# One relu of each unit of the last stage moved from VectorE to ScalarE, in a two-layer bottleneck network

## The chip, the cores and the metric

The kernel runs on one core of a Trainium2 chip. The metric is the device time of one execution in microseconds; the median of three runs of the kernel before is 1983.51 us (1981.97 to 1983.78). The profile is of one further execution of 1982.28 us, with a span of 1980.2 us from the first to the last instruction. Engines are called PE (TensorE, the matrix multiplier; PEld is its weight load), DVE (VectorE), ACT (ScalarE), POOL (GpSimd) and SP (SyncE, which here only queues transfers).

## The reference

Two layers of the same form follow each other, on x of 64 images, 1024 channels, 14 x 14 pixels, in fp32. Each is a bottleneck block with batch statistics taken over the whole batch:

```python
out = jax.nn.relu(_bn(_conv(x, w1, b1, 1, 0), g1, be1))     # 1x1, 1024 -> 256
out = jax.nn.relu(_bn(_conv(out, w2, b2, 1, 1), g2, be2))   # 3x3, 256 -> 256
out = _bn(_conv(out, w3, b3, 1, 0), g3, be3)                # 1x1, 256 -> 1024
out = jax.nn.softplus(residual_scale)[0] * out
out = x + out
return jax.nn.relu(out)
```

The change lies in the last lines of the second layer: third convolution, scale and shift of its normalisation, addition of x, relu, output.

## The kernel before

The batch is cut into T = 32 tiles of two images. A tile of x is 128 partitions x 8 channel blocks x 392 pixels, 1568 KB. The first layer's result lies in device memory (`mid`); the last stage reads it as x, adds the third convolution of the second layer and writes `out`.

The 1x1 convolutions are made with a scheme of seven products in place of eight for a 2 x 2 block of sub-products (`Seven`). In the last stage (`final`, `Conv3Pair`) one **unit** takes a pair of tiles (t, t + 1) and two output channel blocks, `o[0]` = q and `o[1]` = q + 4. Its four results are called (row, i): row picks the channel block, i the tile. A pair has four units (q = 0 to 3), and there are 15 pairs, so 60 units; tile 0 and tile 31 are done by plain products (`residual`) before and after.

A unit has seven products, p1 to p7, of two matmuls each. Three PSUM banks take them: cy (p1, then p6, p7 and p4 added on top), cx (p2), cp (p5, then p3 on top). Between the products the bank is read:

- after p1 and after p6 ACT saves cy, scaled, into the two halves of `cu12`; after p7 into `cu3` (line 438, by way of `act`, line 320);
- DVE adds a scaled bank to x in place (`add`, line 446): (0,0) after p2, (1,1) after p5, (0,1) after p3, (1,0) after p4;
- POOL adds `cu3` to (1,1) (line 467) and the halves of `cu12` to (0,0) and (0,1) (line 493).

So p3 of a unit can't start until DVE has read cp after p5, and p4 not until ACT has read cy after p7.

`stream` (line 294) interleaves each unit with the one before it: p1 of the new unit, p3 and p4 of the old one, then p6 of the new one, then `end()` of the old one, then p2, p5 and p7 of the new one. In `end()` ACT does the relus of row 0, (0,0) and (0,1), with the shift as its bias. The relus of row 1 are in `go_out`, by DVE as add and max in one instruction (line 504). `go_out` is called by the loop `while len(units) > 2` after a later unit's p7, so that a unit is finished two units after its own products. It also queues the unit's two output transfers on SP, one for each tile i, each with two channel blocks (392 KB, line 508).

Before the first unit of a pair DVE makes the column sums t1 to t4 of the pair's inputs (`column_sums`, lines 410 to 413); t1 and t2 have one buffer, t3 and t4 two. x tiles have five buffers. After a pair's second unit the loads of two more tiles are queued (line 1133); each needs a buffer that all four outputs of an earlier tile have left.

The order of ACT's instructions and that of line 504 is held as written (`keep_in_program_order`); the other adds, the column sums, POOL's work and the transfers are placed by the compiler's scheduler.

Of the kernel before, what the change touches and what calls it, by code (L numbers as in the profile page):

```python
# [39 lines left out]
ALU = mybir.AluOpType  # L40
# [47 lines left out]
def bottlenecks(ctx: ExitStack, tc: tile.TileContext, x, w1s, w2s, w3s, pars, out):  # L88
    nc = tc.nc
# [228 lines left out]
    def act(*args, **kw):  # L318

        tc.keep_in_program_order(nc.scalar.activation(*args, **kw))  # L320

    class Conv1(Seven):
# [33 lines left out]
        def end(self):  # L356
            if self.ts[-1] == T - 1 - len(self.ts):
                summarize(self.stats, T // 2 - 1, T - len(self.ts), PX)
# [124 lines left out]
    class Conv3Pair(Conv3):  # L483
# [9 lines left out]
                nc.gpsimd.tensor_add(v, v, self.u12[:, i * self.n : (i + 1) * self.n])  # L493

        def end(self):
            for i in range(2):
                o, v = self.o[0], self.part(0, i)
                act(v, v, AF.Relu, bias=self.shift[:, o : o + 1])

        def go_out(self):  # L500
            for i in range(2):
                o, v = self.o[1], self.part(1, i)
                tc.keep_in_program_order(
                    nc.vector.tensor_scalar(v, v, self.shift[:, o : o + 1], 0.0, ALU.add, ALU.max)  # L504
                )
            q, step = self.o[0], CS // 2
            for i in range(2):
                nc.sync.dma_start(
                    out=self.to[i].rearrange("p (s f) -> p s f", s=CS)[:, q::step, :], in_=self.xt[i][:, q::step, :]
                )  # L510
# [28 lines left out]
    def conv2(psum, pool, b, par, aff, affine_of, stats):  # L539
# [23 lines left out]
        def rows(g, s, k, first, end):  # L563

            return y_grp[:, s, g, 4 * first + k - 1 : 4 * end + k - 4 : 4, :]
# [226 lines left out]
        def finish():  # L792


            for g in range(NG):
# [43 lines left out]
                end = y_grp[:, :, g, H - 1]  # L839
                nc.vector.tensor_add(out_rows[3], d3, fa[:, :, :full])  # L840
                nc.vector.tensor_add(end, d[:, :, full], fa[:, :, full])
                stat(0, [out_rows[3][:, o] for o in range(MS)])
                stat(1, [end[:, o] for o in range(MS)])
# [114 lines left out]
    def gram(psum, pool, homes, aff, minus_c, beside):  # L958
# [17 lines left out]
        def norm_to(end):  # L976

            while pieces and pieces[0][0] < end:
                a, e = pieces.pop(0)
                for s in reversed(range(MS)):  # L980
                    y = y_all[:, s, a:e]
                    if a == 0 and s == 1:
                        norm_vector(s, y, aff, minus_c[:, s : s + 1])
                    else:
                        norm(s, y, aff)
                        less(s, y)
# [422 lines left out]
```

## Time and profile before

| | |
|---|---|
| median of three runs | 1983.51 us |
| profiled span | 1980.2 us |
| PE busy | 1926.9 us, 97% |
| DVE busy | 1582.8 us, 80% |
| ACT busy | 1017.1 us, 51% |
| POOL busy | 540.6 us, 27% |
| granted TensorE clock, mean | 0.991 |

Over the last stage, between 1700 and 1960 us:

| us busy of 260 | PE | DVE | ACT | POOL | DMA share |
|---|---|---|---|---|---|
| | 255.95 | 235.88 | 150.66 | 176.41 | 0.93 |

In that stretch the costliest groups are: DVE line 504, 110 relus, mean 806 ns; DVE line 446, 217 adds, mean about 620 ns; ACT line 320, 164 saves of cy with a mean of 585 ns and 109 relus with a mean of 613 ns; POOL line 493, 109 adds, mean 1042 ns, and line 467, 55 adds, mean 1179 ns.

How to read this: PE's busy share overstates what it does, since matmuls overlap; the distance from one matmul's start to the next says more. A line number can be that of a helper: every ACT instruction of this stage has line 320 and every matmul line 168, so the names of the tiles tell which is which (`x<-x,shift` is a relu, `cu<-cy,scale` a save). In a timeline row, the first number is the start, the second the length of the row (several instructions of one kind make one row, with their count after x), and a bracket gives the idle time of the engine before it and what ended it.

### The profile page before, as it was taken

What the parts mean: (1) busy time and instruction counts of PE and PEld (TensorE: products, weight loads), DVE (VectorE), ACT (ScalarE), POOL (GpSimd) and SP (SyncE); (2) the same over time, 40 slices, a digit from 0 to 9 for tenths busy, and PEclk for the clock granted to TensorE, in tenths of its full rate; (3) what the DMA queues carried; (4) which work ended last, traced back from release to release, by engine and by line L of the source; (5) the groups of instructions that cost most, each with busy time, mean ns of one, the idle gap of its engine ahead of it and who ended that gap; (6) DMA issues with size and microseconds to landing.
All of it is one profiled execution on the core that took longest, in us unless ns stands there. A gap on an engine that the chain in (4) does not pass through costs nothing.

```text
span 1980.2 us, 27057 instructions
## 1 busy us (share of the span) xinstructions
PE 1926.9 (97%) x9432; PEld 1619.1 (82%) x9432; DVE 1582.8 (80%) x2554; ACT 1017.1 (51%) x2039; POOL 540.6 (27%) x638
## 2 busy tenths in 40 slices
PE   8999998999998999999999999989999899999998
PEld 5555557999997789999999999979999887555555
DVE  5778758999997566776776776699999974888997
ACT  1222214677765055555555555447777631555555
POOL 0111100000105133433433433201010060666665
PEclk9999999999999999999999999999999999999999
DMA  7776724676748534444444444257676385799998
GB/s 291 272 255 241 256 98 154 182 209 194 201 138 211 186 131 171 186 165 171 185 165 171 184 167 171 90 183 203 201 192 203 117 209 210 248 330 333 342 335 298
DMA packets 188983, 408.39 MB, mean 206 GB/s; under 512 B 24944, under 2 KB 165136, under 8 KB 172336
## 3 DMA queue, kind: packets, MB, share of 16 engines
q1 hardware_dynamic: 161728, 324.66, 47.8%
q0 software_dynamic: 21504, 30.94, 6.7%
q10 hardware_dynamic: 5616, 51.06, 6.1%
q8 instruction: 75, 1.23, 0.2%
q14 instruction: 60, 0.49, 0.1%
HBM read 263.75 MB, written 115.34 MB: 191 GB/s over the span
## 4 chain that ended last, share of the span: by engine, by line
PE 84%; DVE 10%; DMA 3%; issue 1%; ACT 1%; POOL 0%; DVEq 0%; SPq 0%; ACTq 0%
PE ay L168 17%; PE cy L168 14%; PE columns L168 11%; PE cp L168 11%; PE ap L168 10%; PE m L168 5%; PE l L168 5%; PE ax L168 5%; PE cx L168 4%; DMA x<-mid 2%; DVE x L446 2%; DMA out<-x 1%; PE ps L168 1%; DVE x L504 1%; DVE f L782 1%
## 5 line engine op out<-in xcount | busy, mean ns | idle before, releaser
L320 ACT ACTIVATE cu<-cy,scale 128x196 f32<-128x196 f32 (+1 forms) x552 | 256.9, 474 | 298.7 <-PE cy L168 291.4
L168 PE MATMUL columns<-v,ub 128*128 128x224 f32 (+1 forms) x1536 | 302.1, 338 | 0.7 <-ACT columns L741 0.7
L168 PEld LDWEIGHTS columns<-v,ub 128*128 128x128 f32 x1536 | 270.4, 189 | 4.4 <-ACT columns L741 1.2
L320 ACT ACTIVATE x<-x,shift 128x392 f32<-128x392 f32 x368 | 211.6, 614 | 68.5 <-POOL x L472 52.8
L446 DVE SCALAR_TENSOR_TENSOR x<-cp,scale,x 128x196 f32<-128x196 f32 (+1 forms) x368 | 178.1, 484 | 84.2 <-PE cp L168 81.3
L168 PE MATMUL cy<-ct,ws 128*128 128x196 f32 (+1 forms) x736 | 221.7, 383 | 2.5 <-ACT cu L320 2.5
L467 POOL TENSOR_TENSOR x<-x,cu 128x196 f32<-128x196 f32 (+1 forms) x184 | 167.7, 912 | 170.8 <-ACT cu L320 170.4
L168 PE MATMUL ay<-at,ws 128*128 128x196 f32 (+1 forms) x752 | 209.3, 381 | 1.0 <-ACT au L320 1.0
L472 POOL TENSOR_TENSOR x<-x,cu 128x392 f32<-128x392 f32 x124 | 125.9, 1015 | 190.7 <-DVE x L446 185.9
L168 PEld LDWEIGHTS ay<-at,ws 128*128 128x128 f32 x752 | 136.3, 190 | 35.1 <-ACT au L320 1.9
L168 PEld LDWEIGHTS cy<-ct,ws 128*128 128x128 f32 x736 | 133.6, 190 | 37.0 <-ACT cu L320 4.1
L168 PE MATMUL l<-diffs,ub 128*128 128x224 f32 (+1 forms) x768 | 149.6, 338 | 5.6 <-issue 3.2
L168 PE MATMUL m<-sums,ua 128*128 128x224 f32 (+1 forms) x752 | 145.9, 337 | 3.1 <-DVE sums L607 3.1
L493 POOL TENSOR_TENSOR x<-x,cu 128x392 f32<-128x392 f32 x120 | 125.0, 1042 | 84.1 <-DVE x L446 75.1
L852 POOL DMA_DIRECT2D y<-f x24 | 31.1, 1533 | 411.7 <-DVE f L782 411.7
L168 PEld LDWEIGHTS l<-diffs,ub 128*128 128x128 f32 x768 | 133.7, 189 | 9.6 <-PE columns L168 5.0
L168 PEld LDWEIGHTS m<-sums,ua 128*128 128x128 f32 x752 | 131.3, 189 | 4.9 <-DVE sums L607 4.5
L320 ACT ACTIVATE au<-ay 128x196 f32<-128x196 f32 (+1 forms) x141 | 53.6, 380 | 158.2 <-PE ay L168 157.6
L446 DVE SCALAR_TENSOR_TENSOR x<-cx,scale,x 128x196 f32<-128x196 f32 (+1 forms) x184 | 89.2, 485 | 52.0 <-PE cx L168 51.8
L168 PE MATMUL cy<-y,w 128*128 128x196 f32 (+1 forms) x404 | 126.8, 400 | 0.0
L168 PE MATMUL cx<-y,w 128*128 128x196 f32 (+1 forms) x404 | 125.3, 396 | 0.0
L168 PE MATMUL cp<-zt 128*128 128x257 f32 x392 | 120.1, 388 | 1.7 <-DVE zt L1010 1.7
(203 smaller groups left out, 3990.4 us busy)
## 6 DMA issues: line engine op xcount, KB each, us to landing
x<-in_x SPq DMA_DIRECT2D x62, 1568.0 KB, 6.9
ub<-u SPq DMA_DIRECT2D x94, 768.0 KB, 5.3
x<-mid SPq DMA_DIRECT2D x32, 1568.0 KB, 10.3
mid<-x ACTq DMA_DIRECT2D x31, 1568.0 KB, 5.1
out<-x SPq DMA_DIRECT2D x123, 392.0 KB, 6.9
ua<-u SPq DMA_DIRECT2D x94, 256.0 KB, 3.0
u<-y POOLq DMA_DIRECT2D x48, 256.0 KB, 6.0
home<-y SPq DMA_DIRECT2D x90, 96.0 KB, 4.0
```

The costliest lines, as they stand in the source:

```text
L168: tc.keep_in_program_order(nc.tensor.matmul(*args, **kw))
L320: tc.keep_in_program_order(nc.scalar.activation(*args, **kw))
L446: nc.vector.scalar_tensor_tensor(v, bank, self.scale[:, o : o + 1], v, ALU.mult, ALU.add)
L467: nc.gpsimd.tensor_add(self.part(1, 1), self.part(1, 1), u3)
L472: nc.gpsimd.tensor_add(v, v, self.u12)
L493: nc.gpsimd.tensor_add(v, v, self.u12[:, i * self.n : (i + 1) * self.n])
L504: nc.vector.tensor_scalar(v, v, self.shift[:, o : o + 1], 0.0, ALU.add, ALU.max)
L782: nc.vector.tensor_add(to, v, ls)
L852: nc.gpsimd.dma_start(out=out_rows[0][:, o], in_=f[:, o], accum_op=ALU.add)
```

## The change

The relu of (1,1) leaves `go_out` and DVE and goes to `end()` and ACT, ahead of the two that are there; that of (1,0) stays. It is meant to take work off DVE, which is busier than ACT in this stage.

```diff
         def end(self):
-            for i in range(2):
-                o, v = self.o[0], self.part(0, i)
+            for row, i in (1, 1), (0, 0), (0, 1):
+                o, v = self.o[row], self.part(row, i)
                 act(v, v, AF.Relu, bias=self.shift[:, o : o + 1])
 
         def go_out(self):
-            for i in range(2):
-                o, v = self.o[1], self.part(1, i)
-                tc.keep_in_program_order(
-                    nc.vector.tensor_scalar(v, v, self.shift[:, o : o + 1], 0.0, ALU.add, ALU.max)
-                )
+            o, v = self.o[1], self.part(1, 0)
+            tc.keep_in_program_order(nc.vector.tensor_scalar(v, v, self.shift[:, o : o + 1], 0.0, ALU.add, ALU.max))
             q, step = self.o[0], CS // 2
             for i in range(2):
                 nc.sync.dma_start(
```

## The prediction

> **What bounds the kernel now.** I looked for the stage, then its waits, then the order of work inside one pair of x tiles. The change touches the last stage alone: the VectorE relu of line 504 runs 120 times from 1689.9 to 1967.2 us, two for each of 60 units. The busy table of a stretch that holds exactly 12 pairs (four units each):
>
> ```profile
> 1711.72:1942.93 231.21, 227.30 (x673) 124.63 (x672) 209.70 (x337) 133.07 (x241) 156.16 (x145) 1.00 0.94 332
> ```
>
> Columns: length, PE, PE weight loads, DVE, ACT, POOL, granted clock, DMA share, GB/s. In undisturbed rows of the timeline four matmuls start within 1.32 us, 0.329 each, so 673 need 221.4 of the 231.2 us: PE loses 9.8 us here, 0.82 a pair. DVE is busy 91%, ACT 58%. DMA is busy 231.21 x 0.94 / 12 = 18.1 us a pair; 56 matmuls need 18.42; a pair takes 19.27. So PE leads, and DMA is close behind. Who waits, 1695 to 1960 us (total us, times, longest):
>
> ```profile
> ACT cu L320 <- PE cy L168: 92.0, 88, 2.1
> POOL x L493 <- DVE x L446: 72.4, 79, 1.7
> PEld cp L168 <- DVE x L446: 20.8, 28, 1.4
> ACT x L320 <- POOL x L493: 13.8, 23, 0.9
> ...
> POOL x L493 <- DMA x<-mid: 5.2, 4, 1.3
> ```
>
> The third row costs PE time: twice in each of 14 pairs the weights of p3, which accumulates into bank cp, wait until DVE's add (line 446) after p5 has read that bank. By the last row an x tile came late in 4 pairs. DVE's timeline where the next pair's column sums (lines 410 to 413) fall due:
>
> ```profile
> 1866.03 0.82 DVE L411 TENSOR_TENSOR ct<-ct,y 128x392 f32<-128x392 f32 x1
> 1866.88 0.57 DVE L413 TENSOR_TENSOR ct<-y,ct 128x392 f32<-128x392 f32 x1
> ...
> 1868.44 2.03 DVE L504 TENSOR_SCALAR x<-x,shift 128x392 f32<-128x392 f32 x2
> 1870.39 0.55 DVE L412 TENSOR_TENSOR ct<-y 128x392 f32<-128x392 f32 x1
> 1870.87 0.61 DVE L446 SCALAR_TENSOR_TENSOR x<-cp,scale,x 128x392 f32<-128x392 f32 x1
> 1871.40 0.55 DVE L410 TENSOR_TENSOR ct<-y 128x392 f32<-128x392 f32 x1
> ...
> 1872.95 0.61 DVE L446 SCALAR_TENSOR_TENSOR x<-cp,scale,x 128x392 f32<-128x392 f32 x1
> ```
>
> In other units two relus take 1.14 us and DVE then idles 0.29. Here there are two losses. The first follows lines 411 and 413 with no relu between; by the starts of consecutive matmuls PE loses 0.22 us. The second follows relus of 2.03 us: the p5 add starts at 1872.95 instead of about 1872.17 (p5's matmuls start at 1871.31, and in the undisturbed unit before, matmuls at 1861.87 had their add at 1862.73, 0.86 later), and PE loses 0.41. Over the 14 pairs I count 14 x 0.22 = 3.1 us; nine second losses of about 0.41, 3.7; four of 0.88 to 1.04 where the tile was late as well, 3.8; 0.3 at the end; together 11. The tile's path is in the chain of waits:
>
> ```profile
> 1877.84 0.74 DVE x L504
> 1878.62 5.53 DMA out<-x
> 1884.29 6.63 DMA x<-mid
> 1891.00 1.65 DVE x L446 x3
> ```
>
> A relu frees the output transfer, its landing frees a buffer, the load fills it, and an add of the next pair's first unit uses it. Here the load landed at 1890.92, when the add was just about due: this path has next to no slack. The sync queue:
>
> ```profile
> 1859.54 5.14 SPq L508 DMA_DIRECT2D out<-x  x3
> 1864.85 1.05 SPq L123 DMA_DIRECT2D x<-mid  x2
> 1866.00 17.76 SPq L508 DMA_DIRECT2D out<-x  x8
> ```
>
> In the code the two loads (line 1133) stand ahead of the next unit's two outputs; here they sit between these two. So transfers are queued when they become ready, not as written.
>
> **What the Trainium skill says.** "SBUF — State Buffer", section "Who interferes with whom": a one-source DVE instruction in its two-port mode and a GpSimd instruction exclude each other for the whole instruction; a DVE instruction with two SBUF inputs is excluded by a GpSimd read. The trace agrees: line 504 takes from 0.41 to 1.18 us, mean 0.81, and line 411 takes 0.83 against 0.55 for line 412. "ScalarE: Activation LUTs", section "What ACT_TABLE_LOAD costs": 280 ns + 0.833 ns per element for an activation with a bias column, less some 93 ns back to back, so 606 ns for 392. The trace has 613, and pairs of relus in 1.12: 0.51 for each further one. "VectorE: DVE Perf Modes", section "Mode 2×_2P", lets an fp32 tensor-scalar in SBUF use both ports, which the 0.41 us of the fastest relu fits.
>
> **The change part by part.**
> 1. DVE loses 60 relus, 60 x 0.81 = 48 us of its time, 3.2 a pair. Only what precedes the second loss is on PE's path; elsewhere DVE idles afterwards. There the queue becomes: p5 add, one relu, line 412, p3 add. The saving isn't half of 2.03. GpSimd's add of line 467 runs 1869.10 to 1870.24; line 412 has two SBUF inputs and would now arrive during it, to end at about 1870.6 instead of 1870.94. So the saving is 0.33 us at least, and 1.17 (the second relu whole) if GpSimd isn't in the way. I take 0.33: the p5 add comes at 1872.62, 0.45 late instead of 0.78, and the loss shrinks from 0.41 to 0.08.
> 2. The first loss of 0.22 stays.
> 3. ACT gains 60 relus of 0.51 = 31 us, 58% to 70% of the stage. In an undisturbed unit it runs cu at 1861.42, relus at 1861.90 and 1862.41, and idles 0.37 until cu after p7 at 1863.39. The third relu starts at 1862.92 and ends that slot at 1863.43, so this cu is 0.04 us late. Behind it wait GpSimd's line 467 and PE's p4, whose weights need cu by some 0.2 us after its end: hidden. The relu of (1,1) goes first and waits for line 467 of its unit, done at 1865.29, 1.2 us before its turn: nothing. The relu that waited for GpSimd (13.8 us) is now third, half a microsecond later: no cost.
> 4. Output transfer i = 1 no longer needs DVE. Its last input is the relu of (0,1), ready at about 1863.5 for a unit whose transfer goes out now after the relu of line 504 over a unit later. By the order seen above it will be queued when ready, some 5 us earlier (one unit of 4.6 and a bit), and that tile's buffer is free as much earlier. The first load can take it; it then lands well ahead of its add. The four late tiles lose their excess too: 0.96 becomes 0.08.
>
> Sum: 9 x 0.33 + 4 x 0.88 = 3.0 + 3.5 = 6.5 us. 1983.5 - 6.5 = **1977.0 us**. A pair would then take 18.42 + 0.30 = 18.7 us, above DMA's 18.1. The end (last residual tile on PE, a final output of 1.9 us) keeps its length.
>
> **The rivals.**
> - A, above: 0.62; its bounds for the second loss (0 or 0.2 left) give 1976.0 to 1978.6.
> - E, the first loss goes too, since with less to do DVE runs its sums earlier: all of 10.6 saved, 1973. For it: lines 412 and 410 already run early when inputs allow; against: line 411 starts 0.2 us after the last p6 that read its old value. 0.06.
> - B, the transfers keep their order: loads land just in time as now, and 18.1 us of DMA plus the wait for a landing hold a pair near 19.0. Then about 0.2 us of each of 9 pairs, 1981.7. For it: transfers of 3 to 14 us show a standing backlog. 0.10.
> - C, GpSimd's lock, not the relu, holds DVE: lines 412 and 410 wait as long as the relu did, and only the late tiles improve, 4 x 0.55 = 2.2, 1981.3. 0.06.
> - D, slower. The sync queue has one place in a pair where it stands until a landing, both loads behind it. If the loads come apart, it has two. An output takes 2.8 us from issue to landing at best, but about 1.1 each in a backlog: up to 1.7 us of empty DMA at a wait. With half of that at each of two, a pair takes 18.1 + 1.7 = 19.8 us, 0.5 above today: 14 x 0.5 = 7, 1990.5. For it: DMA's 94%; against: two outputs queued behind the awaited one fill the hole. 0.16.
>
> **How the numbers follow.** 0.2% is 4.0 us, so faster means below 1979.5: nearly all of A, E and a little of B, 0.67. Same: the rest of B and C, and what of A falls short, 0.16. Slower: D and the worst of B, 0.17. The range leaves out D and the far side of E: 1974.0 to 1984.0.
>
> **What would show it.** Right: line 504 x60 and line 320's relu x428; PE's wait of cp weights for line 446 at about 14 large times instead of 28, longest under 0.6; no wait for x<-mid; outputs i = 1 ahead of outputs i = 0; a pair at 18.7 us. Wrong: PE waiting for ACT's cu (0.6 us now), line 412 or 410 growing by what the relu gave up, or long waits of the sync queue for landings with DMA's share falling while x<-mid is late.

## The result and the profile after

The changed kernel takes 1976.78 us, the median of four runs (1975.40 to 1977.39), against 1983.64 us for the kernel before, measured beside it (four runs, 1981.97 to 1984.72). The ratio is 0.9965, with an interval of 0.9948 to 0.9982: faster by 6.9 us, with 3.6 to 10.3 inside the interval. A later repetition gave 1976.81 us against 1982.40, ratio 0.9972 [0.9962, 0.9982]. The forecast was 1977.0.

I read the stage in the same order as before. First the busy table of twelve pairs, the same columns: length, PE, PE weight loads, DVE, ACT, POOL, granted clock, DMA share, GB/s. A pair has 56 matmuls, so a stretch with 672 of them is twelve pairs:

```profile
1711.40:1937.00 225.60, 225.42 (x672) 124.89 (x671) 188.59 (x288) 152.47 (x288) 146.75 (x145) 1.00 0.94 334
```

A pair takes 225.60 / 12 = 18.80 us (19.27 before, 18.7 forecast). DVE is busy 84% of the time (91% before), ACT 68% (58%). DMA's share is the same 0.94, so the same bytes go out in less time.

The waits in the stage, 1690 to 1955 us (total us, times, longest):

```profile
ACT cu L320 <- PE cy L168: 76.7, 56, 1.6
POOL x L493 <- DVE x L446: 65.3, 76, 1.7
DVE x L446 <- PE cp L168: 21.4, 43, 0.6
...
PEld cp L168 <- DVE x L446: 15.6, 28, 0.8
ACT x L320 <- POOL x L493: 4.5, 13, 0.4
PEld cy L168 <- ACT cu L320: 4.1, 13, 0.3
POOL x L493 <- DMA x<-mid: 1.5, 1, 1.5
```

DVE now waits for PE (third row, 43 times; 7.9 us in 27 before), which is how an engine with time to spare looks. PE's wait for DVE before p3 is still there 28 times, twice in each of 14 pairs, but shorter: 15.6 us for 20.8. One x tile came late where four had. The page of the changed kernel has the relu of ACT with its new count, 428 instead of 368:

```profile
L320 ACT ACTIVATE x<-x,shift 128x392 f32<-128x392 f32 x428 | 240.9, 613 | 58.2 <-POOL x L472 52.5
```

DVE's queue where the next pair's column sums fall due, with GpSimd's line 467 and the p5 matmuls between (start, length, engine, line, operation):

```profile
1842.87 0.83 DVE L411 TENSOR_TENSOR ct<-ct,y 128x392 f32<-128x392 f32 x1
1843.73 0.57 DVE L413 TENSOR_TENSOR ct<-y,ct 128x392 f32<-128x392 f32 x1
...
1845.29 0.93 DVE L502 TENSOR_SCALAR x<-x,shift 128x392 f32<-128x392 f32 x1
...
1845.95 1.13 POOL L467 TENSOR_TENSOR x<-x,cu 128x392 f32<-128x392 f32 x1
1846.13 1.38 DVE L412 TENSOR_TENSOR ct<-y 128x392 f32<-128x392 f32 x1
...
1847.43 0.55 DVE L410 TENSOR_TENSOR ct<-y 128x392 f32<-128x392 f32 x1
...
1848.16 0.82 PE L168 MATMUL cp<-ct,ws 128*128 128x392 f32 x2
...
1848.60 2.14 POOL L493 TENSOR_TENSOR x<-x,cu 128x392 f32<-128x392 f32 x2 [1.52 <-DVE x L446]
...
1849.51 0.61 DVE L446 SCALAR_TENSOR_TENSOR x<-cp,scale,x 128x392 f32<-128x392 f32 x1
```

One relu of 0.93 stands where two took 2.03, but line 412 has grown from 0.55 to 1.38: it starts at 1846.13, GpSimd's instruction ends at 1847.08, and line 412 ends 0.43 after that. The p5 add is due at 1848.16 + 0.86 = 1849.02 and starts 0.49 late, where it was 0.78 late before.

From the starts of consecutive matmuls I took, for both traces and every experiment, what PE loses over this stage: all that a distance exceeds 0.329 us, up to the last p4 of the stage, with excesses of some 0.02 us and less left out. Before it is 11.08 us, after 5.83. The first loss of a pair is 0.22 as it was; the second is 0.15 in nearly every pair, for 0.41. The late tile costs 0.45 in place of four at 0.88 to 1.04. The profiled spans differ by 1980.2 - 1974.5 = 5.7 us, so the losses account for nearly all of it.

The late tile in the chain of waits:

```profile
1916.96 7.34 DMA x<-mid
1924.30 0.53 DVE x L446
...
1925.04 0.64 DVE x L446
...
1925.72 0.93 PE cp L168 x2
```

Ahead of this load the chain comes from ACT and PE; it no longer runs back through a relu of DVE and an output transfer. And the sync queue, at the stage's start and in its middle:

```profile
1702.78 0.33 SPq L123 DMA_DIRECT2D x<-mid  x1
1704.69 5.14 SPq L505 DMA_DIRECT2D out<-x  x3
1711.37 0.33 SPq L123 DMA_DIRECT2D x<-mid  x1
...
1841.69 1.05 SPq L123 DMA_DIRECT2D x<-mid  x2
1842.80 17.54 SPq L505 DMA_DIRECT2D out<-x  x8
1860.50 1.05 SPq L123 DMA_DIRECT2D x<-mid  x2
```

In the first pairs the two loads come apart, the first some 5 us ahead of where it stood. From 1724.84 on they leave together again.

### The profile page after: what moved, and what is told of

Its sections match the earlier page's. It is cut to its first block, busy times and chain, and to the rows that moved or that the text cites. A ratio compares the mean times of both kernels' runs of the same rounds, so it can differ in the third digit from the quotient of the medians.

```text
span 1974.5 us, 26993 instructions
## 1 busy us (share of the span) xinstructions
PE 1924.8 (97%) x9432; PEld 1619.0 (82%) x9432; DVE 1556.4 (79%) x2494; ACT 1041.9 (53%) x2099; POOL 529.9 (27%) x638
## 4 chain that ended last, share of the span: by engine, by line
PE 89%; DVE 8%; issue 1%; ACT 1%; DMA 1%; POOL 0%; DVEq 0%; ACTq 0%; SPq 0%
PE cy L168 17%; PE ay L168 17%; PE cp L168 13%; PE columns L168 11%; PE ap L168 10%; PE m L168 5%; PE l L168 5%; PE ax L168 5%; PE cx L168 5%; PE ps L168 1%; DVE v L610 1%; DVE f L779 1%; DVE sums L604 0%; DVE steps L677 0%; DVE steps L573 0%
## 5 line engine op out<-in xcount | busy, mean ns | idle before, releaser
L320 ACT ACTIVATE x<-x,shift 128x392 f32<-128x392 f32 x428 | 240.9, 613 | 58.2 <-POOL x L472 52.5
L467 POOL TENSOR_TENSOR x<-x,cu 128x196 f32<-128x196 f32 (+1 forms) x184 | 159.9, 869 | 172.7 <-ACT cu L320 164.7
```

Source lines behind the costliest of these rows:

```text
L467: nc.gpsimd.tensor_add(self.part(1, 1), self.part(1, 1), u3)
```

## The experiments

Two theories stood at the start. By the one, the gain is DVE's: fewer relus ahead of the p5 add, so PE waits less for bank cp. By the other it is the transfers': the outputs of tile i = 1 need no DVE any more, leave sooner, and the loads land sooner. Later runs ask what limits what is left, and what made ACT's share free. "PE lost" is the sum defined above, from the profiled execution of each kernel; medians are over 5 to 20 executions.

| run | what it is | median us | before beside it | ratio [interval] | PE lost us |
|---|---|---|---|---|---|
| drop11 | after, no relu of (1,1) | 1976.38 | 1982.66 | 0.9969 [0.9958, 0.9981] | 6.39 |
| gate_act | after, output i = 1 held until `go_out` by ACT | 1978.38 | 1982.66 | 0.9977 [0.9969, 0.9985] | 5.88 |
| gate11 | the same, held by DVE | 1978.68 | 1982.66 | 0.9981 [0.9972, 0.9989] | 7.47 |
| after_ct2 | after, t1 and t2 with two buffers | 1986.79 | 1982.66 | 1.0021 [1.0013, 1.0028] | 15.42 |
| spread | the same, one column sum per unit | 1972.92 | 1982.88 | 0.9947 [0.9934, 0.9959] | 1.96 |
| spread_before | the same on the kernel before | 1997.21 | 1982.88 | 1.0067 [1.0053, 1.0081] | 24.34 |
| before_half | before, half of each output transfer | 1979.95 | 1982.88 | 0.9987 [0.9980, 0.9993] | 8.86 |
| both_act | after, both relus on ACT | 1985.46 | 1982.88 | 1.0011 [1.0004, 1.0017] | 13.60 |
| after_again | after | 1976.81 | 1982.40 | 0.9972 [0.9962, 0.9982] | 5.84 |
| last11 | after, relu of (1,1) last | 1982.63 | 1982.40 | 0.9999 [0.9991, 1.0007] | 11.79 |
| spread_again | spread | 1974.23 | 1982.40 | 0.9958 [0.9945, 0.9970] | 2.23 |

The last column minus 11.08, the loss before, matches the difference of the medians within 1.6 us in every row. So to within that, PE's losses in this one stage account for the times of these kernels.

### Does ACT's third relu cost anything? (drop11)

```diff
-            for row, i in (1, 1), (0, 0), (0, 1):
+            for row, i in (0, 0), (0, 1):
```

> The changed kernel with the relu of (1,1) left out on both engines (that quarter of each unit goes out without its shift and relu). If ScalarE's added 31 us are hidden, as predicted, the time stays at that of the changed kernel, 1976.8 us within 1.5. If the third relu costs PE time by a later cu, it falls to 1974 or below, and PE's wait for cu (4.1 us in the changed kernel) goes.

Measured: 1976.38 us. With the relu done nowhere the time is that of the changed kernel (1976.78 and 1976.81), far inside the intervals. PE lost 6.39 us, more than the 5.83 with the relu, because one tile came late by more (a loss of 1.10, where the changed kernel's late tile cost 0.45). ACT's 31 us of added work are hidden.

### Is it the order of the transfers? (gate_act)

A relu of two columns of (1,1), already relued, is put into `go_out` on ACT. It changes no value, but output i = 1 must wait for it, as it did for DVE's relu.

```diff
         def go_out(self):
             o, v = self.o[1], self.part(1, 0)
             tc.keep_in_program_order(nc.vector.tensor_scalar(v, v, self.shift[:, o : o + 1], 0.0, ALU.add, ALU.max))
+            v = self.part(1, 1)[:, :2]
+            act(v, v, AF.Relu)
```

> The changed kernel, and in go_out a relu of two columns of (1,1) on ScalarE, which changes no value: the output transfer i = 1 now has to wait until go_out, as before the change, while VectorE's work stays that of the changed kernel. Theory 1, the gain comes from VectorE having one relu less in front of the second loss: 1977 to 1978.5, second loss near 0.15. Theory 2, the gain comes from output transfers that leave earlier: back to 1980 to 1982, with three or four late x tiles.

Measured: 1978.38 us. PE lost 5.88 us, and the second losses are those of the changed kernel; one late tile cost 0.57. From the second line 411 of the stage to the program's end it took 282.20 us, the changed kernel 282.14, the kernel before 287.53; of the 1.6 us by which its profiled span is longer (1976.1 against 1974.5), 1.5 lie before this stretch. So the gain in the stage is there with the outputs held back, and doesn't need the earlier transfers.

How long before they were needed did the loads land? For 13 pairs in a row, the landing minus the time at which the pair's first p5 add was due (first p5 matmul + 0.86), us, negative is early:

```
before    -2.2 -1.2  1.1  1.2  1.0 -0.4 -0.1 -0.4 -0.1 -0.3 -0.2  1.1  0.0
after     -7.2 -4.8 -3.2 -3.4 -2.5 -1.9 -1.7 -0.6 -0.5 -0.4 -0.7  0.6  0.2
gate_act  -2.6 -2.0 -0.3 -0.7  0.7 -0.6 -0.4  0.1 -0.5  0.2  0.1  0.3 -0.6
```

The changed kernel starts with a lead of 7 us and has nearly used it up by the eighth pair. It is not simply that DMA is too busy to keep a lead: last11 (below) takes 19.3 us a pair at a DMA share of 0.92 and goes from -7.0 to 0.2 over the same eight pairs, while both_act (below), with the same 19.3 us and 0.92 but no output that waits for a relu of DVE, stays between -7.2 and -4.4 throughout. What ends the lead wasn't isolated. gate_act never has a large lead and does as well in this stage.

### The same gate on DVE (gate11)

```diff
+            v = self.part(1, 1)[:, :2]
+            tc.keep_in_program_order(nc.vector.tensor_scalar(v, v, 0.0, None, ALU.max))
```

> The changed kernel, and in go_out a max with 0 of two columns of (1,1) on VectorE behind the relu that stayed; it changes no value. If what the removed relu cost was waiting for GpSimd's instruction to end, two columns cost as much as 392: the second loss returns to about 0.4, 1980 to 1983. If it was the relu's own work, two columns cost next to nothing: 1977 to 1978.5.

Measured: 1978.68 us, just above the second range and far from the first, and PE lost 7.47: the second loss is 0.22 for 0.15, and four tiles were late (losses of 0.30 to 0.76). By the time, the two columns are little work. Their durations tell more. First the instructions of that line over the whole run (shortest, median, longest in ns), then DVE's groups from 1700 to 1960 us (count, busy us, mean ns):

```profile
L504 DVE TENSOR_SCALAR x<-x x60: 154/157/990, 1690.0 to 1962.4; 128x2 f32<-128x2 f32 x60
```

```profile
L504 DVE TENSOR_SCALAR x<-x 128x2 f32<-128x2 f32 x56 | 30.9, 552 | 0.0
...
L412 DVE TENSOR_TENSOR ct<-y 128x392 f32<-128x392 f32 x13 | 7.2, 553 | 0.0
```

and the same group in the changed kernel:

```profile
L412 DVE TENSOR_TENSOR ct<-y 128x392 f32<-128x392 f32 x13 | 17.8, 1373 | 0.0
```

Which duration it is depends on who starts first. In 30 of the 60 units the two columns start some 0.08 us before GpSimd's line 467 and take 154 to 158 ns. In 28 they start 0.05 to 0.19 us after it has begun, and end 0.02 to 0.03 us after it ends, 971 to 990 ns in all. In the pair at 1846 us this instruction starts at 1846.63, line 467 ends at 1847.58, and the two columns end at 1847.605. Line 412, which follows, is then back at 553 ns from 1373. So the wait falls on whichever of these two comes first after line 467 has started; in the kernel before it was the second relu, in the changed one it is line 412. The adds of line 446, which read a PSUM bank, don't wait: the p5 add at 1849.51 in the timeline of the changed kernel takes 0.61 us while line 493 runs, and from 1700 to 1950 us 118 such adds beside GpSimd took 0.61 to 0.63 us, as 94 others did. The Trainium skill has the rule in "SBUF — State Buffer", section "Who interferes with whom": "Issue order, not op shape, decides who blocks", and the two groups of durations agree. The same section has ACT waiting for no other engine over SBUF's ports, and the changed kernel's relus on the two engines agree (shortest, median, longest):

```profile
L502 DVE TENSOR_SCALAR x<-x,shift x60: 410/810/940, 1689.7 to 1960.8; 128x392 f32<-128x392 f32 x60
```

```profile
L320 ACT ACTIVATE x<-x,shift x166: 607/610/623, 1702.5 to 1959.7; 128x392 f32<-128x392 f32 x166
```

### Two buffers for t1 and t2 (after_ct2)

Lines 411 and 413 stand ahead of p3's add with no relu between, since line 411 overwrites a buffer that p6 of the unit before still reads. A second buffer takes that wait away.

```diff
-bufs=2 if i > 1 else 1
+bufs=2 if i > 1 or n == PX else 1
```

> The changed kernel with two buffers for the column sums t1 and t2 of the last stage. The losses left are 14 x 0.22 and 13 x 0.15 us, 5 us, both where the sums fall due. Theory: with a second buffer the sums move into VectorE's idle time and both losses go: about 1972. Rival: at 18.4 us a pair the transfers bind (18.1 us of DMA a pair plus the wait for a landing), and x tiles come late: 1975 or more.

Measured: 1986.79 us, slower than the kernel before. The theory missed; the rival's number (1975 or more) covers it, but not the rival's reason, since no loss here follows a late tile. DVE's timeline shows why:

```profile
1850.38 0.81 DVE L502 TENSOR_SCALAR x<-x,shift 128x392 f32<-128x392 f32 x1
1851.11 0.55 DVE L410 TENSOR_TENSOR ct<-y 128x392 f32<-128x392 f32 x1
1851.59 1.37 DVE L412 TENSOR_TENSOR ct<-y 128x392 f32<-128x392 f32 x1
1852.89 0.55 DVE L411 TENSOR_TENSOR ct<-ct,y 128x392 f32<-128x392 f32 x1
1853.36 0.61 DVE L446 SCALAR_TENSOR_TENSOR x<-cp,scale,x 128x392 f32<-128x392 f32 x1
...
1854.43 1.06 DVE L413 TENSOR_TENSOR ct<-y,ct 128x392 f32<-128x392 f32 x1
...
1855.95 0.61 DVE L446 SCALAR_TENSOR_TENSOR x<-cp,scale,x 128x392 f32<-128x392 f32 x1
```

Freed of their buffer, three sums stand together ahead of the p3 add, and the fourth follows before the p5 add. That add (the last row) was due 0.86 us after the p5 matmuls of 1853.59, at 1854.45, and starts 1.50 late. PE loses 1.05 + 0.10 at this one place of each pair where it had lost 0.22 and 0.15 at two. The wait for the single buffer had kept the sums apart.

### One sum per unit (spread, spread_again)

The same buffers, and the four sums of the next pair placed by hand, one in each unit, behind the add after p4 of the unit before.

```diff
-bufs=2 if i > 1 else 1
+bufs=2 if i > 1 or n == PX else 1
...
+        def one_sum():
+            to, x, y = later.pop(0)
+            op = nc.vector.tensor_add if len(later) == 2 else nc.vector.tensor_sub
+            tc.keep_in_program_order(op(to, x, y))
+
+        def beside():
+            i = next(calls)
+            if i >= 4 and (i - 4) % 6 == 1 and later:
+                one_sum()
...
-        for _ in stream(pairs()):
+        for _ in stream(pairs(), beside):
```

> The changed kernel, with two buffers for t1 and t2 in the last stage, and the four column sums of the next pair put one into each unit, behind the add after p4, where VectorE idles 0.69 us. Theory, the losses left (14 x 0.22 and 13 x 0.15 us) come from sums that fall due together: nearly all 5 us go, 1971.5 to 1973. Rival: at 18.4 us a pair the transfers bind and x tiles come late: 1975 or more.

> The kernel with one column sum in each unit again, beside the changed kernel on one chip: 1972 to 1974, 3 to 4.5 us below the changed kernel if the gain is real; within 2 us of it if the earlier difference was the chip's.

Measured: 1972.92 us, ratio 0.9947 [0.9934, 0.9959], and in the repetition 1974.23, ratio 0.9958 [0.9945, 0.9970], beside 1976.81 for the changed kernel. Both losses are gone from the pairs without a late tile. PE's wait for DVE before p3 (line 449 is this kernel's 446):

```profile
PEld cp L168 <- DVE x L449: 4.1, 6, 1.1
```

Six waits instead of 28; of the 1.96 us still lost, 1.4 follow three late tiles. It is the best version of the study. Its lead over the changed kernel in the repetition is 2.6 us, between the two ranges that were expected (3 to 4.5, and within 2), with intervals that just overlap (0.9962 to 0.9982 against 0.9945 to 0.9970); the profiled losses differ by 3.6 to 3.9.

### The same on the kernel before (spread_before)

The edit is that of spread, on the kernel with two relus on DVE.

> The kernel before, both relus on VectorE, with the column sums spread in the same way. If lumped sums were the cause and the relu only the load that made them hurt, spreading alone saves as much as the change or more: 1973 to 1976. If VectorE with two relus has no room for a sum in each unit (0.29 and 0.69 us idle, 0.55 to 0.83 us needed), the losses spread with it: 1980 or more.

Measured: 1997.21 us, slower by 14 us. DVE's timeline, one unit and the start of the next (L507 is the relu, L1127 a column sum):

```profile
1853.87 2.01 DVE L507 TENSOR_SCALAR x<-x,shift 128x392 f32<-128x392 f32 x2
1855.80 0.61 DVE L449 SCALAR_TENSOR_TENSOR x<-cp,scale,x 128x392 f32<-128x392 f32 x1
1856.34 0.61 DVE L449 SCALAR_TENSOR_TENSOR x<-cy,scale,x 128x392 f32<-128x392 f32 x1
1856.87 1.06 DVE L1127 TENSOR_TENSOR ct<-y,ct 128x392 f32<-128x392 f32 x1
...
1858.92 2.01 DVE L507 TENSOR_SCALAR x<-x,shift 128x392 f32<-128x392 f32 x2
```

With a sum in every unit DVE needs 1858.92 - 1853.87 = 5.05 us for a unit, more than PE's 14 x 0.329 = 4.61, and is busy 259.5 of 260 us. DVE sets the pace, with a loss of 0.35 + 0.10 in nearly every unit. So the moved relu is what makes room for this order, and the two changes are worth together what neither hints at alone.

### What were the late tiles worth? (before_half)

```diff
-                    out=self.to[i].rearrange("p (s f) -> p s f", s=CS)[:, q::step, :], in_=self.xt[i][:, q::step, :]
+                    out=self.to[i].rearrange("p (s f) -> p s f", s=CS)[:, q : q + 1, :], in_=self.xt[i][:, q : q + 1, :]
```

> The kernel before with half of its output transfers: of each unit only the channel blocks of row 0 go out, so that DMA has 15 us a pair or less (the other half of the output isn't written). If late x tiles make a good part of what the change saved, this saves it too: late tiles vanish, 1980.5 to 1981.5 with the second losses of 0.41 left. If transfers hardly matter, it stays at 1982.5 within 1.

Measured: 1979.95 us, ratio 0.9987 [0.9980, 0.9993], half a microsecond below the range that was expected. With DMA's share down to 0.68 between 1700 and 1960 us, loads land 4.5 to 6.1 us early throughout, no tile is late, and every second loss is 0.30 + 0.10. PE lost 8.86, 2.2 less than before. So lateness was worth 2.2 us by the losses and 2.9 by the medians, and DVE's part of the loss stays whatever DMA does.

### Does ACT have room for both? (both_act)

```diff
-            for row, i in (1, 1), (0, 0), (0, 1):
+            for row, i in (1, 1), (0, 0), (0, 1), (1, 0):
...
-            o, v = self.o[1], self.part(1, 0)
-            tc.keep_in_program_order(nc.vector.tensor_scalar(v, v, self.shift[:, o : o + 1], 0.0, ALU.add, ALU.max))
```

> The changed kernel with the relu of (1,0) on ScalarE as well, fourth in end(): no relu on VectorE. By the timeline the cu after p7 would come 0.55 us late in each unit, and p4's weights have about 0.3 us to spare: PE loses about 0.25 us in each of 60 units, 1976.8 + 15 = about 1990, with PE waiting for cu. If ScalarE's room of 70% is what counts, it stays at 1976 or below, since VectorE's second loss goes.

Measured: 1985.46 us, ratio 1.0011 [1.0004, 1.0017]: all of the gain lost and a little more, by the path that was expected and with a little over half of the expected cost (8.7 of 15 us). Now the weights of cy wait for ACT's save of the bank:

```profile
PEld cy L168 <- ACT cu L320: 35.9, 96, 0.7
```

ACT is busy 193.9 of 260 us there, 75%, and yet its queue is too long: four relus take 2.15 us in one go, and the two saves of cy behind them come late, 0.07 + 0.10 of PE in two of a pair's four units and 0.25 + 0.10 in a third. DVE's part of the loss did shrink, to 0.11 + 0.10 once a pair.

### Does the place of the moved relu matter? (last11, after_again)

```diff
-            for row, i in (1, 1), (0, 0), (0, 1):
+            for row, i in (0, 0), (0, 1), (1, 1):
```

> The changed kernel with the relu of (1,1) third in end() instead of first. The order before had ScalarE wait 13.8 us for GpSimd's line 493 in front of the relu of (0,1); in the changed kernel that relu is third and the wait 4.5 us. Theory: ScalarE's waits are off the path, so the place doesn't matter: 1976.8 within 1.5, with the wait for line 493 back above 10 us. Rival: placing it first is part of the gain: 1979 or more.

> The changed kernel itself, for comparison on the same chip with the next two: 1976.8 us within 1.5; ratio to the kernel before 0.9965 within 0.001.

Measured: 1982.63 us, ratio 0.9999 [0.9991, 1.0007], with the changed kernel at 1976.81 beside it. The rival holds: the whole gain is gone, by the place of one entry in a list, while DVE's order of instructions is the same. ACT's wait for line 493 is back at 11.5 us, as the theory said, but it isn't off the path. The timeline in a pair's first unit (brackets: idle time before, and what ended it):

```profile
1852.79 0.61 ACT L320 ACTIVATE x<-x,shift 128x392 f32<-128x392 f32 x1
...
1853.21 2.14 POOL L493 TENSOR_TENSOR x<-x,cu 128x392 f32<-128x392 f32 x2 [1.52 <-DMA x<-mid]
...
1854.26 1.14 ACT L320 ACTIVATE x<-x,shift 128x392 f32<-128x392 f32 x2 [0.85 <-POOL x L493]
...
1855.30 1.04 ACT L320 ACTIVATE cu<-cy,scale 128x392 f32<-128x392 f32 x2
...
1855.92 0.93 PE L168 MATMUL cy<-ct,w 128*128 128x392 f32 x2 [0.21 <-ACT cu L320]
```

The relu of (0,1) waits 0.85 us for GpSimd's add, the first of the two in the POOL row, which starts 0.44 us after the p5 matmuls (1852.77) as it does in the changed kernel (1848.60 and 1848.16). (The bracket of the POOL row names a DMA; DVE's add after p3 ended at 1853.12, just before it too.) The relu of (1,1), whose input has long been there, stands behind it; then come the saves, and PE's p4 waits for one. In the changed kernel the relu of (1,1) fills that hole, ACT idles 0.34 instead of 0.85, and no loss follows. The new loss is 0.37 + 0.10 in twelve pairs and smaller in two (0.33 and 0.15): 6.2 us, somewhat more than the 5.25 that the change had won by the losses.

## Why the prediction was right, and where its steps were off

- **Step 1, the second loss.** Right in kind and in the queue: one relu, then line 412 meeting GpSimd's line 467. The p5 add comes 0.49 late, forecast 0.45. Mis-sized was the loss that follows, 0.15 instead of 0.08. The losses have two parts that the forecast's subtraction didn't keep apart: the wait itself (0.30 before, 0.04 now) and 0.10 between the two matmuls after the wait, which came with nearly every such wait at any length. A wait made short keeps its 0.10. Twelve such pairs cost 12 x 0.07 = 0.8 us more than forecast.
- **Step 2, the first loss.** Stayed at 0.22, as forecast. spread shows it could go.
- **Step 3, ACT.** Free, as forecast (drop11). But of its clauses the one that looked least, that the relu waiting for GpSimd is now third and costs nothing, is what all hangs on: behind that wait, the moved relu takes the whole gain back (last11). The condition was in the diff's order and the forecast treated it as a detail.
- **Step 4, transfers.** Half right. The loads did come earlier than before, by 5.0 us at first (forecast: some 5), but by 1.6 in the seventh of the 13 pairs and hardly after that, and gate_act shows that the stage keeps its gain without it. One late tile of four remained, 0.45 instead of 0.08. What this step booked as a gain from transfers, 3.5 us, contains the relief of DVE in those four pairs (4 x 0.26); lateness by itself was worth 2.2 us (before_half). Why gate_act, with loads as tight as before, had fewer late tiles than before isn't settled: its worst landing is 0.7 late against 1.0 to 1.2 in four pairs of the kernel before, and I didn't isolate what makes that difference.
- **The sum.** By the losses: 9 x (0.41 - 0.15) = 2.3, and 4 x (0.96 - 0.15) = 3.2, less 0.3 for the late tile that is left: 5.2, where the forecast had 6.5. The traces have 11.08 - 5.83 = 5.25. Of this, 13 x 0.26 = 3.4 is DVE's shorter queue, which drop11, gate_act and before_half show; the other 1.9 is the late tiles that are gone, and why they go even in gate_act stays open. The median moved by 6.9 and by 5.6, and an interval of 3.6 to 10.3 can't tell 5.2 from 6.5, so it is in part luck that the forecast median is nearer than its steps are.
- **Rival C** (GpSimd's lock holds DVE) was right in its mechanism: line 412 went from 0.55 to 1.37, and took back 13 x 0.82 = 10.7 us of DVE's freed time. Its size was wrong: one relu and line 412 take 2.22 us (1845.29 to 1847.51), where two relus and line 412 took 2.50 (1868.44 to 1870.94), so the p5 add still gains 0.28.
- **Rival D** (loads that come apart leave DMA empty) named an event that happened, in the first pairs, without the harm: DMA's share stayed at 0.94. **B** (loads just in time, a pair near 19.0 us) was right on the loads from the eighth pair on and wrong on the pair, which takes 18.8 there too. **E** (the first loss goes too) failed, since that loss stayed; removing it took a different order of the sums and not only a less busy DVE.
- **What would show it**: the counts of instructions came out as said. Two signs of being wrong came up in part and did no harm: line 412 grew (rival C), and PE's wait for ACT's cu went from 0.6 to 4.1 us. One wait for x<-mid was left. The 28 waits for cp did not become 14: all stayed, with a mean of 15.6 / 28 = 0.56 us and a longest of 0.8 where under 0.6 was forecast. A weight load that waits is seen before PE itself loses time: the waits before p3 in the last11 trace are 0.58 and 0.51 us where the distance of matmuls shows 0.12 and 0.04 lost, so some 0.46 of each is free, and this view couldn't show a loss of 0.3 shrink to 0.04.

## What to carry to other kernels

When work moves between engines, ask where in the receiving queue it lands: ahead of an instruction that must wait, in time that was idle anyway, it is free; behind that wait it pushes everything after it. Short of 100% an engine's share of busy time decided nothing here, since ACT at 75% held PE up (both_act) and DVE at 85% nearly not (spread). And once an engine has room, the order of its remaining work is worth a second look: the same rearrangement cost 14 us before the move and won 2.6 after it.

## What the runs showed of the hardware

- A wait of DVE for GpSimd did not depend on the size of DVE's instruction: 2 columns took 157 ns when they started first and up to 990 ns when GpSimd's add had, and the instruction behind them fell from 1373 to 553. Taking one waiter away handed the wait to the next. DVE's adds that read a PSUM bank took 0.61 us beside GpSimd, so they are not among the waiters.
- After PE had waited for a bank, its next two matmuls started 0.43 us apart instead of 0.329 in nearly every case, whether the wait was 0.04 or 0.94 us.
- Three executions of much the same queue (before, changed, gate_act) had loads landing from 7.2 us early to 1.2 us late with DMA busy near 94%, so which tile is late there isn't read from that share.
